# Layers 2 and 3's constants moved from VectorE to GpSimd and ScalarE, and two units' layer-1 attention split by batch, in a four-layer graph kernel

## The chip, the core and the metric

One core of one Trainium2 chip. The metric is the device time of one execution in microseconds. In the profile PE is TensorE's matmuls, PEld its weight loads, DVE is VectorE, ACT ScalarE, POOL GpSimd and SP the sync engine, which here only issues DMAs. L12 is line 12 of the kernel before.

## What is computed

`x` is (64, 256, 128) in float32: 64 batches of 256 nodes with 128 features. `adj` is one symmetric 256x256 matrix of zeros and ones. Four layers follow, each `x = layernorm(x + layer(x))`, all in float32.

```python
# layer 0
h = x @ others_weight;  e = leaky_relu(u1[idx1] + u2[idx2], 0.1)   # u1 = h@a1, u2 = h@a2
out = softmax(where(adj > 0, e, -9e15), axis=1) @ h + x @ self_weight
# layer 1
h = x @ W;  e = leaky_relu(h@a_src + (h@a_dst).T, 0.2)
out = elu(softmax(where(adj + I == 0, -1e9, e)) @ h)
# layer 2: five gated steps; in_matrix = out_matrix = adj
m = adj @ h;  av = concat(m, m);  u3 = h @ u3_w.T + u3_b
z = sigmoid(av @ w3_w.T + w3_b + u3);  r = sigmoid(av @ w4_w.T + w4_b + u3)
hv = tanh(av @ w5_w.T + w5_b + (r*h) @ u5_w.T + u5_b);  h = (1-z)*h + z*hv
# layer 3: y = sum of adj^k x, k = 0..3, twice (adj0 = adj1 = adj), each with its own weight
```

## The kernel before

The batches are taken in 32 units of two (`UB = 2`). A unit's working tile is 128 partitions by 512 values. Ten units are in flight at once, each in a lane with its own SBUF tiles; eight PSUM banks of 128x512 are shared.

No engine's order of work is written by hand. Every instruction is handed to a planner with `add(engine, ns, function, reads, writes)`, where `ns` is a guess of its duration. `Plan.run` plays the engines forward in time on these guesses: when an engine comes free it takes, of the instructions whose inputs are there by the plan, the one with the smallest key. The key (`first`, L996) is the unit's number times 43 us plus the instruction's due time within the unit; due times are the guessed durations and latencies along the unit, stretched by `PACE` (3.1; 1.56 in layer 2). Constants have a rank instead: 0, `R2 = 1` or `R3 = 1.5` times 43 us. The order that comes out is fixed in the program; on the chip each engine goes through its own list in order and waits where an input is late.

Constants (L338 to L498) are made by the same queues while the first units begin: `adjT` (transposed adjacency), `neg0` and `mask1` for the softmaxes; then, of rank R2, the gate weights `gs` (three sums and a difference, L438 and L441) which TensorE transposes into `gT` (L442), the biases `bias2` (L446, L448), the adjacency in another node order `adj_p` (L452), and `fast_blocks` (L461), which makes from `adjTp` and from `adjT` eight 128x128 blocks each, four of them copied (L469) and four of them sums and differences (L471, L474, L475). `left_fast` (L798) multiplies with these blocks, seven products in place of eight. Of rank R3 are layer 3's weights `w3` (L484, L486).

Layer 0 (L620): `x` must lie features by nodes. For units below `XDIRECT = 8` it is loaded as it stands and turned by four TensorE transposes and a ScalarE copy (`feature_major`, L520); later units are loaded by four DMAs in a pattern that one VectorE transpose (L625) turns. A row of attention terms must reach all partitions: for units below `DIRECT_ROWS = 3`, `on_all` (L557) does that with four TensorE transposes into PSUM, later units write a row to DRAM and read it back to all partitions; the same choice decides how the term `d` is made (four one-column products at L663, or two DMAs at L654). Then come masked scores (L669 to L677), their maxima (L679, and `s` at L682), Exp with row sums (L687), the scaling of `h` (L696 for units 0 to 3) and the products L709 and L714, then a layernorm: statistics on VectorE (L577), a power on GpSimd (L582), the scaling (L603 to L613).

Layer 1 (L727): four Prelus on ScalarE (L733, one for each batch and half of the nodes), one Exp over both batches (L736), one multiply with `mask1` over both (L737), the products L744 into one bank, one ScalarE copy (L747), the products L757, reciprocals and scaling (L761 to L768), elu (L774 to L786), layernorm. After unit 0's last scaling, six dummy products (`warm`) are planned at the lowest rank.

Layer 2 (L846) has TensorE's largest share: five products of 512 columns in each of its steps (L868), and `left_fast` (L811) or the plain product (L794). Layer 3 (L948) has L969 and L976.

The helper `small` (L510) sends some short instructions of units from `TIGHT = 4` up to GpSimd, those named in `SMALL`, with a planned 220 ns, and the others to VectorE.

Of the kernel before, what the change touches and what calls it, by code (L numbers as in the profile page):

```python
# [9 lines left out]
AF = mybir.ActivationFunctionType  # L10
# [3 lines left out]
P = 128  # L14
# [7 lines left out]
FAST = (1, 2, 3, 4, 5)  # L22
NORM = (0, 1, 2, 3)
SCALES = True
SMALL = ("ve", "cu", "d", "s", "elu", "shift")
TIGHT = 4
FIRST_FAR = {0: 2, 1: 2}
LAST_FAR = {0: 1}
PERIOD = 43e3
TAIL = 0.3  # L30
LATE = 6
PACE = 3.1
PACE_GATED = 1.56
HOLD = 80
DIRECT_ROWS = 3
XDIRECT = 8
START = 35e3
R2 = 1
R3 = 1.5
# [158 lines left out]
def kernel(  # L198
# [28 lines left out]
    nc = tc.nc  # L227
# [207 lines left out]

    gs = [cell(f"gs{k}", [D, D]) for k in range(3)]
    for k in range(3):
        add(DVE, 250, lambda k=k: nc.vector.tensor_add(gs[k].ap, gates[k].ap[:, 0, :], gates[k].ap[:, 1, :]),  # L438
            (gates[k],), (gs[k],))

    add(DVE, 250, lambda: nc.vector.tensor_sub(gs[0].ap, gs[0].ap, gs[1].ap), (gs[0], gs[1]), (gs[0],))  # L441
# [6 lines left out]
    add(DVE, 150, lambda: nc.vector.tensor_scalar_mul(bias2.ap[:, 0:2], bias2.ap[:, 0:2], 0.5), (bias2,), (bias2,))  # L448
# [12 lines left out]
    def fast_blocks(name, mat):  # L461


        f = cell(name, [P, 2 * NC, N])

        def block(k):
            return f.ap.rearrange("p k (c n) -> p (k c) n", c=NC)[:, k]

        add(DVE, 420, lambda: nc.vector.tensor_copy(f.ap[:, 0:NC], mat.ap), (mat,), (f,))  # L469
        for out, (i, op, j) in {4: (1, ALU.subtract, 0), 6: (3, ALU.add, 1), 5: (6, ALU.subtract, 0)}.items():  # L470
            add(DVE, 250, lambda out=out, i=i, op=op, j=j: nc.vector.tensor_tensor(block(out), block(i), block(j), op=op),  # L471
                (f,), (f,))

        add(DVE, 250, lambda: nc.vector.tensor_scalar_mul(block(5), block(5), -1.0), (f,), (f,))  # L474
        add(DVE, 250, lambda: nc.vector.tensor_add(block(7), block(5), block(2)), (f,), (f,))  # L475
        return f

    adjTf = fast_blocks("adjTf", adjTp)
# [2 lines left out]

    plan.rank = R3
    w3 = cell("w3", [D, 2, 2, D])
    add(DVE, 250, lambda: nc.vector.tensor_add(w3.ap[:, 0, 0, :], wk.ap[:, :, 0], ident.ap), (wk, ident), (w3,))  # L484
# [85 lines left out]
    def layernorm(u, L, pairs, swap=False, centred=False, last=False):  # L570
# [14 lines left out]
        if by_act and not centred:  # L585
            mean = st.ap.rearrange("p k (j s) -> p k j s", j=2)[:, :, :, 1]
            if "shift" in SMALL:
                add(POOL, 220, lambda: nc.gpsimd.tensor_scalar_mul(
                    nm.ap.rearrange("p (k j) -> p k j", k=2), mean, -1.0), (st,), (nm,))
                add(POOL, 220, lambda: nc.gpsimd.tensor_mul(ve.ap, nm.ap, rstd.ap), (nm, rstd), (ve,))  # L590
# [136 lines left out]
    def layer1(u, L):  # L727
        H = D + 1
        esd, e, p = L["esd"], L["e"], L["p"]
        es, ev = on_all(u, L["m"], L["row"], esd, lambda: esd.ap[:, 0])  # L730
        for g in range(G):
            b = g // NC
            add(ACT, 600, lambda g=g, b=b: nc.scalar.activation(  # L733
                e.ap[:, g, :].rearrange("p (c n) -> p c n", c=NC), ev()[:, b], AF.Prelu, bias=esd.ap[:, 1, g : g + 1], alpha=0.2), (es, esd), (e,), group=es)
        ef, pf = e.ap.rearrange("p g n -> p (g n)"), p.ap.rearrange("p g n -> p (g n)")
        add(ACT, 950, lambda: nc.scalar.activation(ef, ef, AF.Exp), (e,), (e,))  # L736
        add(DVE, 1150, lambda: nc.vector.tensor_mul(  # L737
            p.ap.rearrange("p (b c) n -> p b (c n)", b=UB), e.ap.rearrange("p (b c) n -> p b (c n)", b=UB),
            mask1.ap.rearrange("p (o c) n -> p o (c n)", o=1).to_broadcast([P, UB, NC * N])), (e, mask1), (p,))

        ps_x, px = bank(), L["xT0"]
        for b in range(UB):
            for jc in range(NC):
                add(PE, mm_ns(N), lambda b=b, jc=jc: nc.tensor.matmul(  # L744
                    ps_x.ap[:, b * N : (b + 1) * N], X[u].ap[:, b, jc, :], p.ap[:, b * NC + jc, :],
                    start=(b == 0 and jc == 0), stop=(jc == NC - 1), skip_group_check=True), (X[u], p), (ps_x,))
        add(ACT, 500, lambda: nc.scalar.copy(px.ap, ps_x.ap), (ps_x,), (px,))  # L747
        rs, hp, hn, th = L["rs"], L["ht"], L["m"], L["th"]
        ex, parts = L["ex"], object()
        for b in range(UB):  # L750
            ps_o = bank()

            def ov(ps_o=ps_o):
                return ps_o.ap[:, 0 : NC * H].rearrange("p (c k) -> p c k", c=NC)

            for ic in range(NC):
                add(PE, mm_ns(H), lambda b=b, ic=ic, ov=ov: nc.tensor.matmul(  # L757
                    ov()[:, ic, :], bn(px.ap)[:, b, ic * P : (ic + 1) * P], wx1.ap,
                    start=(ic == 0), stop=True, skip_group_check=True), (px, wx1), (ps_o,))
            r = rs.ap[:, b * NC : (b + 1) * NC].rearrange("p (c o) -> p c o", o=1)  # L760
            add(DVE, 120, lambda r=r, ov=ov: nc.vector.reciprocal(r, ov()[:, :, D : D + 1]), (ps_o,), (rs,), group=parts)  # L761
            for c in range(NC if SCALES and u >= TIGHT else 0):
                add(ACT, 290, lambda b=b, c=c, ov=ov: nc.scalar.activation(
                    gd(hp.ap)[:, b * NC + c, :], ov()[:, c, 0:D], AF.Copy, scale=rs.ap[:, b * NC + c : b * NC + c + 1]),
                    (ps_o, rs), (hp,), group=parts)
            if not SCALES or u < TIGHT:
                add(DVE, 350, lambda b=b, r=r, ov=ov: nc.vector.tensor_mul(
                    gd(hp.ap)[:, b * NC : (b + 1) * NC, :], ov()[:, :, 0:D], r.to_broadcast([P, NC, D])), (ps_o, rs), (hp,), group=parts)  # L768
# [267 lines left out]
```

## Time and profile before

| | us |
|---|---|
| median of 7 runs | 1400.63 |
| lowest and highest | 1399.58, 1401.84 |
| the profiled execution's own time | 1400.57 |
| its span in the profile | 1398.8 |
| TensorE busy in the span | 1385.7 |
| VectorE busy | 1206.2 |
| ScalarE busy | 932.7 |
| GpSimd busy | 281.7 |

The span runs from the first instruction to the last of the profiled execution. The granted TensorE clock was 0.999 of full speed. The DMA queues moved 147.05 MB. A row of the groups by line reads: line, engine, operation, tiles written and read, shapes, count, busy us, mean ns, and the idle time of that engine just before these instructions with what ended most of it. "x8" of a float32 matmul is four matmuls, since each is recorded twice, while a transpose is recorded once.

### The profile page before, as it was taken

What the parts mean: (1) busy time and instruction counts of PE and PEld (TensorE: products, weight loads), DVE (VectorE), ACT (ScalarE), POOL (GpSimd) and SP (SyncE); (2) the same over time, 40 slices, a digit from 0 to 9 for tenths busy, and PEclk for the clock granted to TensorE, in tenths of its full rate; (3) what the DMA queues carried; (4) which work ended last, traced back from release to release, by engine and by line L of the source; (5) the groups of instructions that cost most, each with busy time, mean ns of one, the idle gap of its engine ahead of it and who ended that gap; (6) DMA issues with size and microseconds to landing.
All of it is one profiled execution on the core that took longest, in us unless ns stands there. A gap on an engine that the chain in (4) does not pass through costs nothing.

```text
span 1398.8 us, 21934 instructions
## 1 busy us (share of the span) xinstructions
PE 1385.7 (99%) x6529; PEld 962.5 (69%) x6529; DVE 1206.2 (86%) x2849; ACT 932.7 (67%) x2147; POOL 281.7 (20%) x526
## 2 busy tenths in 40 slices
PE   8999999999999999999999999999999999999998
PEld 8767676767666666676766676776666666666776
DVE  7978898989989989889889898899789888899853
ACT  5897756465675767766676678788765546565543
POOL 0312011112212212221221221133112011112212
PEclk9999999999999999999999999999999999999999
DMA  4214455445545544555445645545454443455512
GB/s 118 64 38 101 98 113 126 93 103 121 123 100 119 117 106 103 125 110 117 111 102 115 128 99 124 112 106 126 94 121 115 101 107 85 108 119 120 116 45 53
DMA packets 533254, 147.05 MB, mean 105 GB/s; under 512 B 460688, under 2 KB 498320, under 8 KB 533136
## 3 DMA queue, kind: packets, MB, share of 16 engines
q1 hardware_dynamic: 532336, 145.13, 46.3%
q8 instruction: 52, 0.85, 0.3%
q14 instruction: 66, 0.54, 0.1%
q10 hardware_dynamic: 800, 0.52, 0.1%
HBM read 81.10 MB, written 64.46 MB: 104 GB/s over the span
## 4 chain that ended last, share of the span: by engine, by line
PE 96%; DVE 2%; ACT 1%; issue 0%; POOL 0%; ACTq 0%; POOLq 0%; DVEq 0%
PE ps L868 48%; PE ps L811 17%; PE ps L969 8%; PE ps L794 5%; PE ps L744 4%; PE ps L714 4%; PE ps L976 4%; PE ps L757 2%; PE ps L709 2%; PE ps L638 2%; ACT p L687 0%; PE ps L345 0%; DVE e L669 0%; PE ps L523 0%; PE ps L933 0%
## 5 line engine op out<-in xcount | busy, mean ns | idle before, releaser
L868 PE MATMUL ps<-m,gT 128*128 128x512 f32 x960 | 462.6, 592 | 0.0
L868 PEld LDWEIGHTS ps<-m,gT 128*128 128x128 f32 x960 | 171.9, 190 | 127.0 <-issue 104.9
L887 ACT ACTIVATE e<-ps,bias 128x512 f32<-128x512 f32 x160 | 110.6, 691 | 122.3 <-PE ps L868 122.0
L879 ACT ACTIVATE e<-ps,bias 128x512 f32<-128x512 f32 x160 | 110.2, 689 | 104.2 <-PE ps L868 102.6
L582 POOL TENSOR_TENSOR rstd<-ve,nhalf 128x4 f32<-128x4 f32 x128 | 144.9, 1133 | 94.0 <-DVE ve L579 91.3
L868 PE MATMUL ps<-e,u5T 128*128 128x512 f32 x320 | 162.9, 592 | 0.0
L811 PEld LDWEIGHTS ps<-adjTf,ht 128*128 128x128 f32 x726 | 115.8, 191 | 65.6 <-issue 55.0
L579 POOL TENSOR_SCALAR ve<-st 128x4 f32<-128x4 f32 x112 | 36.2, 323 | 589.1 <-DVE st L577 543.4
L811 PE MATMUL ps<-adjTf,e 128*128 128x128 f32 x968 | 138.4, 275 | 0.0
L896 ACT ACTIVATE p<-ps,bias 128x512 f32<-128x512 f32 x160 | 110.0, 689 | 42.5 <-PE ps L868 39.3
L811 PEld LDWEIGHTS ps<-adjTf,e 128*128 128x128 f32 x968 | 125.4, 192 | 13.6 <-issue 11.6
L811 PE MATMUL ps<-adjTf,ht 128*128 128x128 f32 x726 | 122.4, 274 | 0.0
L898 DVE SCALAR_TENSOR_TENSOR p<-e,p 128x512 f32<-128x512 f32 x160 | 109.3, 684 | 14.2 <-ACT p L896 13.7
L868 PEld LDWEIGHTS ps<-e,u5T 128*128 128x128 f32 x320 | 59.6, 190 | 65.8 <-issue 52.1
L868 PE MATMUL ps<-xT,gT 128*128 128x512 f32 x192 | 97.4, 593 | 0.0
L838 DVE TENSOR_TENSOR m<-ps,e 128x256 f32<-128x256 f32 x152 | 63.4, 417 | 39.1 <-PE ps L811 36.2
L733 ACT ACTIVATE e<-m,esd 128x256 f32<-128x256 f32 x116 | 83.4, 766 | 0.7 <-DMA m<-row 0.7
L823 ACT COPY e<-ps 128x128 f32<-128x128 f32 x152 | 39.9, 266 | 55.1 <-PE ps L811 50.7
L536 DVE STREAM_TRANSPOSE p<-x 128x512 f32<-128x512 f32 x61 | 67.5, 1106 | 7.5 <-ACT x L603 7.0
L577 DVE BATCH_NORM_STATS2 st<-ps 128x6 f32<-128x256 f32 x128 | 51.9, 423 | 25.1 <-PE ps L976 15.0
L841 DVE TENSOR_TENSOR m<-ps,m 128x256 f32<-128x256 f32 x152 | 63.1, 417 | 11.0 <-PE ps L811 9.3
L714 PEld LDWEIGHTS ps<-ht,p 128*128 128x128 f32 x512 | 64.7, 190 | 11.4 <-issue 10.8
(189 smaller groups left out, 2904.1 us busy)
## 6 DMA issues: line engine op xcount, KB each, us to landing
hb<-p SPq DMA_DIRECT2D x182, 256.0 KB, 2.3
ht<-hb SPq DMA_DIRECT2D x484, 64.0 KB, 2.5
xT<-hb SPq DMA_DIRECT2D x244, 64.0 KB, 2.6
m<-row SPq DMA_DIRECT2D x58, 256.0 KB, 3.8
hb<-p SPq DMA_DIRECT2D x124, 64.0 KB, 1.8
ht<-hb SPq DMA_DIRECT2D x31, 256.0 KB, 3.1
out_dram<-x SPq DMA_DIRECT2D x29, 256.0 KB, 2.4
m<-in_x_dram SPq DMA_DIRECT2D x96, 64.0 KB, 2.3
```

The costliest lines, as they stand in the source:

```text
L536: add(DVE, 1050, lambda: nc.vector.transpose(v.ap.rearrange("p (a g i) -> p g a i", g=G, i=BL), X[u].ap.rearrange("p b c (j a) -> p (b c) ...
L582: add(POOL, 1050, lambda: nc.gpsimd.tensor_tensor(rstd.ap, ve.ap, nhalf.ap, op=ALU.pow), (ve, nhalf), (rstd,))
L714: add(PE, mm_ns(D + 2), lambda b=b, ic=ic, kc=kc, yv=yv: nc.tensor.matmul(yv()[:, ic, :], p.ap[:, b * NC + kc, ic * P : (ic + 1) * P], h.a ...
L733: add(ACT, 600, lambda g=g, b=b: nc.scalar.activation(e.ap[:, g, :].rearrange("p (c n) -> p c n", c=NC), ev()[:, b], AF.Prelu, bias=esd.ap ...
L794: add(PE, mm_ns(N), lambda b=b, mc=mc: nc.tensor.matmul(ps.ap[:, b * N : (b + 1) * N], lhs(b, mc), mat.ap[:, mc, :], start=(mc == 0), stop ...
L811: add(PE, mm_ns(P) + 4, lambda: nc.tensor.matmul(ps.ap[:, at * P : (at + 1) * P], lhs(), mat.ap[:, k, c * P : (c + 1) * P], start=True, st ...
L868: add(PE, mm_ns(T), lambda: nc.tensor.matmul(ps.ap, w(), rhs.ap, start=start, stop=stop, skip_group_check=True), (c, rhs), (ps,), after)
L879: add(ACT, 600, lambda ps_g=ps_g, up=up: nc.scalar.activation(r.ap, ps_g.ap, AF.Tanh, bias=bias2.ap[:, 1:2], scale=0.5 / up), (ps_g, bias2 ...
L887: add(ACT, 600, lambda ps_g=ps_g, up=up: nc.scalar.activation(z.ap, ps_g.ap, AF.Tanh, bias=bias2.ap[:, 0:1], scale=0.5 / up), (ps_g, bias2 ...
L896: add(ACT, 600, lambda ps_v=ps_v, up=up: nc.scalar.activation(v.ap, ps_v.ap, AF.Tanh, bias=bias2.ap[:, 2:3], scale=1 / up), (ps_v, bias2), ...
L898: add(DVE, 600, lambda: nc.vector.scalar_tensor_tensor(v.ap, z.ap, 1.0, v.ap, op0=ALU.add, op1=ALU.mult), (v, z), (v,))
L969: add(PE, mm_ns(N), lambda k=k, src=src, c=c, b=b: nc.tensor.matmul(view(c)[:, :, b, :], bn(src.ap)[:, b, c * P : (c + 1) * P], w3.ap[:, k ...
```

## The change

Four parts, and the planner's numbers with them.

1. The 22 instructions that make `gs`, `bias2`, the summed blocks of `fast_blocks` and `w3` are on GpSimd instead of VectorE; the three copies (`adj_p`, and the first half of each `fast_blocks`) are on ScalarE.
2. In layer 1, units 0 and 1 (`HALVES = 2`) go batch by batch: Prelus, Exp, mask, products, copy for batch 0, then for batch 1, each batch with a PSUM bank of its own. Other units do as before.
3. `s` (L682) is no longer in `SMALL`, so it is on VectorE for all units. `DIRECT_ROWS` is 4 instead of 3 and `XDIRECT` 9 instead of 8: unit 3 gets its rows and `d` by TensorE, unit 8 its `x` by TensorE.
4. `PACE` is 2.8 instead of 3.1, and the planned costs of short GpSimd instructions rise from 220 to 250, 280 or 300 ns.

```diff
-SMALL = ("ve", "cu", "d", "s", "elu", "shift")
+SMALL = ("ve", "cu", "d", "elu", "shift")
+HALVES = 2
-PACE = 3.1
+PACE = 2.8
-DIRECT_ROWS = 3
-XDIRECT = 8
+DIRECT_ROWS = 4
+XDIRECT = 9
...
-        add(DVE, 250, lambda k=k: nc.vector.tensor_add(gs[k].ap, gates[k].ap[:, 0, :], gates[k].ap[:, 1, :]),
+        add(POOL, 480, lambda k=k: nc.gpsimd.tensor_add(gs[k].ap, gates[k].ap[:, 0, :], gates[k].ap[:, 1, :]),
...
-        add(DVE, 150, lambda k=k, j=j: nc.vector.tensor_add(
+        add(POOL, 270, lambda k=k, j=j: nc.gpsimd.tensor_add(
...
-    add(DVE, 600, lambda: nc.vector.tensor_copy(
+    add(ACT, 600, lambda: nc.scalar.copy(
         adj_p.ap, adj_t.ap.rearrange("p i (m q j) -> p (i m) j q", m=NC, j=BL)), (adj_t,), (adj_p,))
...
-        add(DVE, 420, lambda: nc.vector.tensor_copy(f.ap[:, 0:NC], mat.ap), (mat,), (f,))
+        add(ACT, 500, lambda: nc.scalar.copy(f.ap[:, 0:NC], mat.ap), (mat,), (f,))
...
-            add(DVE, 250, lambda out=out, i=i, op=op, j=j: nc.vector.tensor_tensor(block(out), block(i), block(j), op=op),
+            add(POOL, 480, lambda out=out, i=i, op=op, j=j: nc.gpsimd.tensor_tensor(block(out), block(i), block(j), op=op),
...
-        add(DVE, 350, lambda k=k: nc.vector.tensor_add(
+        add(POOL, 480, lambda k=k: nc.gpsimd.tensor_add(
             w3.ap[:, k % 2, k // 2, :], wk.ap[:, :, k], wk.ap[:, :, k + 3]), (wk,), (w3,))
...
-        add(POOL if pool else DVE, 220 if pool else ns, lambda: op(nc.gpsimd if pool else nc.vector), reads, writes, **more)
+        add(POOL if pool else DVE, 300 if pool else ns, lambda: op(nc.gpsimd if pool else nc.vector), reads, writes, **more)
...
+        for bs in [[b] for b in range(UB)] if u < HALVES else [list(range(UB))]:
+            n = len(bs)
+            ec, pc = (e, p) if n == UB else ((L["r"], L["v"]), (L["z"], L["xT1"]))[bs[0]]
...
+            add(ACT, 115 + 418 * n, lambda at=at: nc.scalar.activation(e.ap[:, at], e.ap[:, at], AF.Exp), (ec,), (ec,))
+            add(DVE, 50 + 550 * n, lambda at=at, n=n: nc.vector.tensor_mul(
...
+            ps_x = bank()
...
+            add(ACT, 80 + 210 * n, lambda bs=bs, n=n, ps_x=ps_x: nc.scalar.copy(
+                px.ap[:, bs[0] * N : bs[0] * N + n * N], ps_x.ap[:, 0 : n * N]), (ps_x,), (px,), group=copies)
```

The same moves are made for the lines that are left out (the difference `gs`, the scaling of `bias2`, the negation and the last sum of `fast_blocks`, the first block of `w3`). Within a batch of layer 1 the products and the scaling are the lines of before.

More of the change, by code (lines that the diff above doesn't have):

```diff
@@ L437 @@
     for k in range(3):
-        add(DVE, 250, lambda k=k: nc.vector.tensor_add(gs[k].ap, gates[k].ap[:, 0, :], gates[k].ap[:, 1, :]),
+        add(POOL, 480, lambda k=k: nc.gpsimd.tensor_add(gs[k].ap, gates[k].ap[:, 0, :], gates[k].ap[:, 1, :]),
             (gates[k],), (gs[k],))
-    add(DVE, 250, lambda: nc.vector.tensor_sub(gs[0].ap, gs[0].ap, gs[1].ap), (gs[0], gs[1]), (gs[0],))
+    add(POOL, 480, lambda: nc.gpsimd.tensor_sub(gs[0].ap, gs[0].ap, gs[1].ap), (gs[0], gs[1]), (gs[0],))
     gT = transposed("gT", [(gs[0], gs[0].ap), (gs[1], gs[1].ap), (gs[2], gs[2].ap), (u3, u3.ap)])
@@ L445 @@
     for k, j in enumerate((3, 3, 4)):
-        add(DVE, 150, lambda k=k, j=j: nc.vector.tensor_add(
+        add(POOL, 270, lambda k=k, j=j: nc.gpsimd.tensor_add(
             bias2.ap[:, k : k + 1], biases.ap[:, k : k + 1], biases.ap[:, j : j + 1]), (biases,), (bias2,))
-    add(DVE, 150, lambda: nc.vector.tensor_scalar_mul(bias2.ap[:, 0:2], bias2.ap[:, 0:2], 0.5), (bias2,), (bias2,))
+    add(POOL, 300, lambda: nc.gpsimd.tensor_scalar_mul(bias2.ap[:, 0:2], bias2.ap[:, 0:2], 0.5), (bias2,), (bias2,))
     adjTp, adj_p = cell("adjTp", [P, NC, N]), cell("adj_p", [P, NC * NC, BL, P // BL])
-    add(DVE, 600, lambda: nc.vector.tensor_copy(
+    add(ACT, 600, lambda: nc.scalar.copy(
         adj_p.ap, adj_t.ap.rearrange("p i (m q j) -> p (i m) j q", m=NC, j=BL)), (adj_t,), (adj_p,))
@@ L467, in block @@
             return f.ap.rearrange("p k (c n) -> p (k c) n", c=NC)[:, k]
-        add(DVE, 420, lambda: nc.vector.tensor_copy(f.ap[:, 0:NC], mat.ap), (mat,), (f,))
+        add(ACT, 500, lambda: nc.scalar.copy(f.ap[:, 0:NC], mat.ap), (mat,), (f,))
         for out, (i, op, j) in {4: (1, ALU.subtract, 0), 6: (3, ALU.add, 1), 5: (6, ALU.subtract, 0)}.items():
-            add(DVE, 250, lambda out=out, i=i, op=op, j=j: nc.vector.tensor_tensor(block(out), block(i), block(j), op=op),
+            add(POOL, 480, lambda out=out, i=i, op=op, j=j: nc.gpsimd.tensor_tensor(block(out), block(i), block(j), op=op),
                 (f,), (f,))
-        add(DVE, 250, lambda: nc.vector.tensor_scalar_mul(block(5), block(5), -1.0), (f,), (f,))
-        add(DVE, 250, lambda: nc.vector.tensor_add(block(7), block(5), block(2)), (f,), (f,))
+        add(POOL, 350, lambda: nc.gpsimd.tensor_scalar_mul(block(5), block(5), -1.0), (f,), (f,))
+        add(POOL, 480, lambda: nc.gpsimd.tensor_add(block(7), block(5), block(2)), (f,), (f,))
         return f
@@ L483 @@
     w3 = cell("w3", [D, 2, 2, D])
-    add(DVE, 250, lambda: nc.vector.tensor_add(w3.ap[:, 0, 0, :], wk.ap[:, :, 0], ident.ap), (wk, ident), (w3,))
+    add(POOL, 480, lambda: nc.gpsimd.tensor_add(w3.ap[:, 0, 0, :], wk.ap[:, :, 0], ident.ap), (wk, ident), (w3,))
     for k in range(1, 4):
-        add(DVE, 350, lambda k=k: nc.vector.tensor_add(
+        add(POOL, 480, lambda k=k: nc.gpsimd.tensor_add(
             w3.ap[:, k % 2, k // 2, :], wk.ap[:, :, k], wk.ap[:, :, k + 3]), (wk,), (w3,))
@@ L587, in layernorm @@
             if "shift" in SMALL:
-                add(POOL, 220, lambda: nc.gpsimd.tensor_scalar_mul(
+                add(POOL, 280, lambda: nc.gpsimd.tensor_scalar_mul(
                     nm.ap.rearrange("p (k j) -> p k j", k=2), mean, -1.0), (st,), (nm,))
-                add(POOL, 220, lambda: nc.gpsimd.tensor_mul(ve.ap, nm.ap, rstd.ap), (nm, rstd), (ve,))
+                add(POOL, 250, lambda: nc.gpsimd.tensor_mul(ve.ap, nm.ap, rstd.ap), (nm, rstd), (ve,))
             else:
@@ L730, in layer1 @@
         es, ev = on_all(u, L["m"], L["row"], esd, lambda: esd.ap[:, 0])
[L731 to L768, printed above, removed]
@@ new lines, in layer1, with ov @@
+        px, rs, hp, hn, th, ex = (L[name] for name in ("xT0", "rs", "ht", "m", "th", "ex"))
+        parts, copies = object(), object()
+        for bs in [[b] for b in range(UB)] if u < HALVES else [list(range(UB))]:
+            n = len(bs)
+            ec, pc = (e, p) if n == UB else ((L["r"], L["v"]), (L["z"], L["xT1"]))[bs[0]]
+            at = slice(bs[0] * NC, (bs[-1] + 1) * NC)
+            for b in bs:
+                for g in range(b * NC, (b + 1) * NC):
+                    add(ACT, 600, lambda g=g, b=b: nc.scalar.activation(
+                        e.ap[:, g, :].rearrange("p (c n) -> p c n", c=NC), ev()[:, b], AF.Prelu,
+                        bias=esd.ap[:, 1, g : g + 1], alpha=0.2), (es, esd), (ec,), group=es)
+            add(ACT, 115 + 418 * n, lambda at=at: nc.scalar.activation(e.ap[:, at], e.ap[:, at], AF.Exp), (ec,), (ec,))
+            add(DVE, 50 + 550 * n, lambda at=at, n=n: nc.vector.tensor_mul(
+                p.ap[:, at].rearrange("p (b c) n -> p b (c n)", b=n), e.ap[:, at].rearrange("p (b c) n -> p b (c n)", b=n),
+                mask1.ap.rearrange("p (o c) n -> p o (c n)", o=1).to_broadcast([P, n, NC * N])), (ec, mask1), (pc,))
+            ps_x = bank()
+            for k, b in enumerate(bs):
+                for jc in range(NC):
+                    add(PE, mm_ns(N), lambda b=b, jc=jc, k=k, ps_x=ps_x: nc.tensor.matmul(
+                        ps_x.ap[:, k * N : (k + 1) * N], X[u].ap[:, b, jc, :], p.ap[:, b * NC + jc, :],
+                        start=(k == 0 and jc == 0), stop=(jc == NC - 1), skip_group_check=True), (X[u], pc), (ps_x,))
+            add(ACT, 80 + 210 * n, lambda bs=bs, n=n, ps_x=ps_x: nc.scalar.copy(
+                px.ap[:, bs[0] * N : bs[0] * N + n * N], ps_x.ap[:, 0 : n * N]), (ps_x,), (px,), group=copies)
+            for b in bs:
+                ps_o = bank()
+                def ov(ps_o=ps_o):
+                    return ps_o.ap[:, 0 : NC * H].rearrange("p (c k) -> p c k", c=NC)
+                for ic in range(NC):
+                    add(PE, mm_ns(H), lambda b=b, ic=ic, ov=ov: nc.tensor.matmul(
+                        ov()[:, ic, :], bn(px.ap)[:, b, ic * P : (ic + 1) * P], wx1.ap,
+                        start=(ic == 0), stop=True, skip_group_check=True), (px, wx1), (ps_o,))
+                r = rs.ap[:, b * NC : (b + 1) * NC].rearrange("p (c o) -> p c o", o=1)
+                add(DVE, 120, lambda r=r, ov=ov: nc.vector.reciprocal(r, ov()[:, :, D : D + 1]), (ps_o,), (rs,), group=parts)
+                for c in range(NC if SCALES and u >= TIGHT else 0):
+                    add(ACT, 290, lambda b=b, c=c, ov=ov: nc.scalar.activation(
+                        gd(hp.ap)[:, b * NC + c, :], ov()[:, c, 0:D], AF.Copy, scale=rs.ap[:, b * NC + c : b * NC + c + 1]),
+                        (ps_o, rs), (hp,), group=parts)
+                if not SCALES or u < TIGHT:
+                    add(DVE, 350, lambda b=b, r=r, ov=ov: nc.vector.tensor_mul(
+                        gd(hp.ap)[:, b * NC : (b + 1) * NC, :], ov()[:, :, 0:D], r.to_broadcast([P, NC, D])),
+                        (ps_o, rs), (hp,), group=parts)
```

## The prediction

> **What bounds the kernel.** I read the page's engine shares first, then the chain that ended last, then the busy table by stretches of the start, then TensorE's waits, and last the timeline around the longest of those waits.
>
> ```profile
> PE 1385.7 (99%) x6529; PEld 962.5 (69%) x6529; DVE 1206.2 (86%) x2849; ACT 932.7 (67%) x2147; POOL 281.7 (20%) x526
> PE 96%; DVE 2%; ACT 1%; issue 0%; POOL 0%; ACTq 0%; POOLq 0%; DVEq 0%
> 10.00:20.00 10.00, 9.28 (x79) 8.64 (x79) 8.05 (x36) 6.17 (x20) 0.00 (x0) 1.00 0.80 193
> 20.00:30.00 10.00, 8.28 (x72) 7.85 (x71) 9.11 (x32) 6.59 (x20) 1.24 (x2) 1.00 0.10 17
> 30.00:40.00 10.00, 10.00 (x80) 9.71 (x79) 9.54 (x30) 7.28 (x24) 3.73 (x7) 1.00 0.21 28
> 40.00:50.00 10.00, 8.89 (x48) 6.95 (x48) 9.09 (x31) 7.29 (x21) 4.29 (x7) 1.00 0.31 85
> ```
>
> The columns of the stretches are PE, PEld, DVE, ACT and POOL busy us, granted clock, DMA share, GB/s. TensorE is busy 99% and carries 96% of the last chain; VectorE's 86% is no bound of the whole. Only in the first 60 us does TensorE have gaps, and there VectorE is at 8 to 9.5 of 10 us while POOL does almost nothing.
>
> A busy TensorE could still run slowly, so I looked at the distance between the starts of consecutive matmuls: 112 ns for 128 columns, 216 for 256, 429 for 512, everywhere (in the timeline, eight L709 matmuls take 0.89 us and eight L969 ones 1.73). Those distances, summed over all 6529 matmuls, are about 1381 us. So the span is work 1381, plus about 3 us before the first DMA lands (four dummy products run there anyway), some stalls, and about 6.8 us from the last matmul (1392.0) to the end (1398.8). The stalls, from the same starts, are 5.6 us between 4.4 and 60 us and 3.3 us in all that follows (the largest 1.36 us at 338.6). No engine speedup can win more than these 8.9 us unless it takes TensorE work away.
>
> ```profile
> PE ps L744 <- DVE p L737: 2.8, 2, 1.7
> PE ps L345 <- POOL ident masks.py:199: 1.3, 1, 1.3
> PE ps L757 <- ACT xT L747: 1.2, 1, 1.2
> PE ps L523 <- DVE adjf L471: 0.4, 1, 0.4
> PE ps L523 <- DMA m<-in_x_dram: 0.3, 1, 0.3
> ```
>
> The waits name the line (total us, times, longest). The largest is L744, layer 1's first product, behind the mask multiply L737: once for unit 0 and once for unit 1. Its run-up in the timeline, unit 0:
>
> ```profile
> 25.54 1.57 ACT L733 ACTIVATE e<-ps,esd 128x256 f32<-128x256 f32 x4 [0.28 <-ACT ht L641]
> 27.14 1.06 ACT L736 ACTIVATE e<-e 128x1024 f32<-128x1024 f32 x1
> 28.40 1.22 DVE L737 TENSOR_TENSOR p<-e,mask 128x1024 f32<-128x1024 f32 x1
> 29.67 1.99 PE L744 MATMUL ps<-p,x 128*128 128x256 f32 x8 [1.72 <-DVE p L737]
> ```
>
> Four Prelus, one Exp over both batches, one multiply over both, and only then may TensorE start: 4.1 us in series.
>
> **The change, part by part.**
>
> *Halves, units 0 and 1.* One batch needs two Prelus (0.79), an Exp of 512 (0.62, row L780), a multiply of 512 (two-input row L786: 0.69): from 25.54 the first product could start near 27.75 instead of 29.67. TensorE came free at 27.8, so that stall of 1.98 us (with its 0.1 us of refill) goes, and what is late next is the second batch: ScalarE is through its Exp near 28.4, VectorE near 29.1, while the first batch's four matmuls end near 28.6. I leave 0.45 us of stall: saved 1.5. At 46.15, unit 1, the stall was 1.37; by the same arithmetic I leave 0.3: saved 1.1. The price is a shorter second instruction of each kind: two Exps for one, 2 x 0.62 - 1.06 = 0.18 us per unit; two multiplies, 2 x 0.69 - 1.22 = 0.16; two PSUM copies, 2 x 0.38 (row L641, 266 columns) - 0.58 = 0.18. All of it lies within the shorter series above. TensorE's matmuls stay the same.
>
> *Constants.* 25 VectorE instructions leave: by the busy column L438 0.8, L441 0.3, L446 and L448 0.6, L452 0.6, L469 0.8, L471 1.8, L474 0.4, L475 0.6, L484 and L486 1.4, together 7.3 us, all between 5.5 and 26.9 us. ScalarE takes three 512-wide copies, about 0.6 each (row L378): 1.8 us, in stretches where it is 3.5 to 6.2 of 10 us busy; without that cover they would cost at most 1.8 on the way to the first layer. POOL takes 22. The trace has no 128x128 two-input POOL instruction: the nearest row below is the one-input select of the identity at 0.29 us, the longest POOL row of any kind is 2.71 (L582). I take 0.5 for each of 18 wide ones, near the lower row because beside no other work POOL's rows lie at their minima, and 0.2 for the four bias ones: 10 us, between 8 and about 25 us, where POOL was busy 1.2 us. First uses: gT at 45.7, adjTf at 99.6, adjf at 162, w3 at 175.6, so 20 us of cover at least, except that gs is transposed on TensorE at 15.2, in order. Behind these on POOL stands rstd L582 of unit 0 at 21.8; at most one 0.5 us instruction stands before it.
> What does 7.3 us less on VectorE bring? Not 7.3. Between 10 and 20 us the first unit's series is latency: VectorE is 8 of 10 us busy and the instructions that stand in its way there are a 0.4 copy at 11.4, gT at 15.9, a bias and a block at 17.4. TensorE's stalls at 16.1 and 17.0 (0.48 and 0.56) and the small ones (about 1.3 with that near 58) are what can be won; I take 0.7 and 0.4 of them. Bounds: nothing, and 2.3.
>
> *Unit 3's rows by TensorE.* Added: four transposes for layer 0 and four for layer 1, 8 x 0.112 = 0.9 us, and four one-column products (eight records; 24 records took 2.3 us) 0.8. Removed: seven SP DMAs with their two round trips (L550, L554, L654), 1.2 us of ScalarE (L733 from PSUM 474 ns against 762 from SBUF, four times), 0.4 of VectorE (L669 417 against 608, twice). *Unit 8's x by TensorE:* four transposes 0.45 us and a 0.59 ScalarE copy, against a 0.69 VectorE transpose and four SP issues that become one. TensorE's total grows by 2.1 us, and since it is the bound, this is paid in full unless it fills a stall that would have stayed; VectorE and SP gain where they are not the limit.
>
> *s back on VectorE for units 4 up.* 56 POOL instructions of a median 556 ns go, 56 of 227 ns come to VectorE, 12.7 us over the run, of which 2.7 for units 4 to 9 before 90 us.
>
> ```profile
> L682 POOL TENSOR_SCALAR s<-top,d x56: 259/556/1815, 45.7 to 1229.3; 128x2 f32<-128x2 f32 x56
> L682 DVE TENSOR_SCALAR s<-top,d x8: 223/226/234, 12.2 to 44.7; 128x2 f32<-128x2 f32 x8
> ```
>
> Minimum, median and longest: POOL's instruction stretches beside VectorE, VectorE's does not. Cost nothing: TensorE has no stall between 59 and 250 us. Without that cover it would be up to 2.7.
>
> *The planner's numbers* (PACE 2.8, POOL costs 250 to 300). They reorder every queue. The 3.3 us of later stalls are places where the written order and the real times differ; I keep 3.3, between nothing and twice that. The end of 6.8 us is a fixed series of statistics, power, scaling and store.
>
> **Sum.** The profiled execution took 1400.57, its span 1398.8, so 1.8 lies around it; the median is 1400.63. 1400.6 - 1.5 - 1.1 - 0.7 - 0.4 + 2.1 = 1399.0.
>
> **The rivals.**
> *More is won.* All 5.6 us at the start go and a third of the later 3.3: 1400.6 - 5.6 - 1.1 + 2.1 = 1396.0. For it: every stall at the start stands behind VectorE, ScalarE or a late load, all relieved. Against: each unit 2 up still has the unsplit series (stall of 0.35 at 57.5).
> *GpSimd is late, slower.* TensorE takes its instructions in order, and the transposes of gs (L364) are written in near 15 us. If the six or so POOL instructions up to gs take 1.8 us each (the longest L682) instead of 0.5, TensorE stands 6 x 1.3 = 8 us: 1399.0 + 8 = 1407. It ends slower than before by 0.2% once they take over about 1.25 us each. Against: the long POOL rows lie beside dense two-input VectorE work such as L737 and L898, of which little is left before 15 us.
> *VectorE is held by GpSimd.* Beside POOL work VectorE's rows keep their length (L898 684 ns with, 685 without), but POOL's were tiny there. If all 18 wide ones held VectorE for their 0.5, it would lose 9 and win 7.3: the stalls stay and the series grows by 1.7: 1400.6 + 2.1 + 1.7 = 1404.4; it turns from gain to loss where 7.3 us are lost. The Trainium skill, SBUF — State Buffer, "Who interferes with whom", says that a VectorE instruction with two SBUF inputs or in a two-port mode and a GpSimd one that reads SBUF exclude each other for the whole instruction, whichever starts first; the stretched POOL rows agree with one half of that, and no row here shows the other half.
> *The new order is worse.* Later stalls double: 1399.0 + 3.3 = 1402.3; triple: 1405.6. Against: the POOL costs in the plan come nearer to the rows (220 before, median 556).
>
> **Chances.** Forecast 0.52, more won 0.31, GpSimd late 0.04, VectorE held 0.04, worse order 0.09. A measurement of this kernel can tell about 0.2%, 2.8 us: faster is under 1397.8, slower over 1403.4. Faster: 0.31 and 0.03 of the forecast's lower edge, 0.34; slower: 0.08 and half of the worse order, 0.12; same 0.54. The range, 1395.3 to 1402.6, takes in the bounds of the start (all of it gone, none of the rest) and the worse order once; it leaves out the two GpSimd cases and its tripling.
>
> **What would show it.** Halves right: L744's wait behind the multiply under 1 us for units 0 and 1 and its first start near 27. Constants right: POOL about 10 us busy before 30 us, VectorE's share there lower, rows near 0.5. TensorE's extra work: 20 more matmul records. The stalls to 60 us near 2 us. It would be wrong if the gs transposes had a wait on POOL, or if L757 or L868 in later stretches had waits that sum to more than 5 us.

## The result, and the profile after

The changed kernel takes 1396.54 us in the median (1395.85 to 1398.13, 14 runs), the kernel before 1400.55 (34 runs): ratio 0.9973, 95% interval 0.9966 to 0.998. That is 4.0 us faster where 1.6 was forecast; 1399.0 was predicted in a range of 1395.3 to 1402.6. The profiled execution's span fell from 1398.8 to 1394.9.

From here on, views of the changed kernel and of those made from it have the lines of that kernel: a line up to layer 1 (L727) stands one further down (L687 is L688), layer 1's L733, L736, L737, L744, L747 and L757 are L741, L744, L745, L752, L755 and L764, and what follows in layers 2 and 3 is eight further down (L868 is L876). Kernels made from the kernel before keep its lines, except before_halves_only, which has those of the changed kernel.

The page of the changed kernel, its engines and its last chain:

```profile
PE 1386.4 (99%) x6549; PEld 965.7 (69%) x6549; DVE 1208.4 (87%) x2880; ACT 937.0 (67%) x2155; POOL 257.3 (18%) x492
PE 99%; ACT 0%; POOL 0%; DVE 0%; issue 0%; ACTq 0%; POOLq 0%; DVEq 0%
```

The 20 added matmul records are there, and VectorE's 2% of the last chain is gone (the share of the span that each engine has in the chain of work that ended last). The stretches of its start (PE, PEld, DVE, ACT, POOL busy us, clock, DMA share, GB/s):

```profile
10.00:20.00 10.00, 9.87 (x87) 9.54 (x87) 8.73 (x27) 6.07 (x19) 8.15 (x20) 1.00 0.84 213
20.00:30.00 10.00, 9.70 (x85) 9.41 (x84) 7.59 (x28) 6.50 (x21) 1.03 (x1) 1.00 0.00 1
30.00:40.00 10.00, 10.00 (x74) 9.56 (x73) 9.42 (x32) 7.99 (x22) 3.37 (x5) 1.00 0.01 2
40.00:50.00 10.00, 10.00 (x46) 7.04 (x46) 5.47 (x18) 7.93 (x25) 0.39 (x2) 1.00 0.16 36
```

TensorE is nearly full from 10 us on and POOL has taken the constants. VectorE is less busy than before from 20 to 30 us (7.59 instead of 9.11) but not from 10 to 20 (8.73 instead of 8.05). All waits of TensorE that its table names, in the whole run:

```profile
PE ps L346 <- POOL ident masks.py:199: 1.3, 1, 1.3
PE ps L664 <- ACT ht L642: 0.3, 1, 0.3
```

The first is the start, before any work. Every other wait of the kernel before is gone, those late in the run too (L757 behind L747). Busy time in long stretches shows the same: TensorE fills all 1320 us, where before it had 239.90, 298.71, 400.00 and 379.74.

```profile
60.00:300.00 240.00, 240.00 (x1112) 164.44 (x1111) 218.66 (x528) 165.01 (x372) 31.45 (x49) 1.00 0.42 94
300.00:600.00 300.00, 300.00 (x1400) 205.78 (x1399) 266.75 (x630) 208.99 (x487) 60.40 (x107) 1.00 0.52 113
600.00:1000.00 400.00, 400.00 (x1909) 280.15 (x1908) 355.56 (x831) 303.46 (x706) 81.87 (x163) 1.00 0.53 114
1000.00:1380.00 380.00, 380.00 (x1703) 256.53 (x1702) 319.20 (x735) 214.86 (x475) 61.18 (x122) 1.00 0.44 100
```

**One account for all kernels.** I take from each trace the distance between the starts of consecutive matmuls and subtract the usual one of its form (111.5 ns for 128 columns, 112 for 129 and 130, 113.5 for 133, 216 for 256, 429.3 for 512, and 118 for up to two columns). What is left is stall; it is summed from 7.3 us, where the clock is full in every profile, and the sum is split at 62 us. The usual distances alone are TensorE's work, and the tail runs from the last matmul to the end. Before: work 1381.0, stalls 5.3 to 62 us and 2.8 later, tail 6.5. After: 1383.3, 0.7, 0 (-0.1), 6.9. (The prediction's 5.6 and 3.3 counted only the gaps over 60 ns of the same list.) The change in span is therefore +2.3 - 4.6 - 2.9 + 0.4, and +0.9 in the first 7.3 us, where the granted clock of this one execution was half until 6.8 us and that of the kernel before until 4.4 (see the end): -3.9. Without these first microseconds the account would give -4.8; the medians differ by 4.0.

### The profile page after: what moved, and what is told of

The parts are those of the page before. It is cut to its first block, busy times and chain, and to the rows that moved or that the text cites. A ratio compares the mean times of both kernels' runs of the same rounds, so it can differ in the third digit from the quotient of the medians.

```text
span 1394.9 us, 21958 instructions
## 1 busy us (share of the span) xinstructions
PE 1386.4 (99%) x6549; PEld 965.7 (69%) x6549; DVE 1208.4 (87%) x2880; ACT 937.0 (67%) x2155; POOL 257.3 (18%) x492
## 4 chain that ended last, share of the span: by engine, by line
PE 99%; ACT 0%; POOL 0%; DVE 0%; issue 0%; ACTq 0%; POOLq 0%; DVEq 0%
PE ps L876 49%; PE ps L819 17%; PE ps L977 8%; PE ps L802 5%; PE ps L715 4%; PE ps L752 4%; PE ps L984 4%; PE ps L764 2%; PE ps L710 2%; PE ps L639 2%; PE ps L346 0%; PE ps L524 0%; PE ps L567 0%; PE ps L941 0%; PE ps L664 0%; ACT p L688 0%
## 5 line engine op out<-in xcount | busy, mean ns | idle before, releaser
L876 PE MATMUL ps<-m,gT 128*128 128x512 f32 x960 | 464.3, 592 | 0.0
L876 PEld LDWEIGHTS ps<-m,gT 128*128 128x128 f32 x960 | 171.5, 190 | 119.9 <-issue 97.5
L876 PE MATMUL ps<-e,u5T 128*128 128x512 f32 x320 | 163.1, 592 | 0.0
L906 DVE SCALAR_TENSOR_TENSOR p<-e,p 128x512 f32<-128x512 f32 x160 | 109.5, 685 | 11.0 <-ACT p L904 10.1
L876 PEld LDWEIGHTS ps<-e,u5T 128*128 128x128 f32 x320 | 59.9, 190 | 61.0 <-issue 47.1
L876 PE MATMUL ps<-xT,gT 128*128 128x512 f32 x192 | 96.7, 593 | 0.0
L741 ACT ACTIVATE e<-m,esd 128x256 f32<-128x256 f32 x112 | 80.7, 766 | 0.0
L890 DVE SCALAR_TENSOR_TENSOR e<-e,xT 128x512 f32<-128x512 f32 x96 | 65.4, 682 | 13.6 <-ACT e L887 12.2
L715 PEld LDWEIGHTS ps<-ht,p 128*128 128x128 f32 x512 | 66.0, 190 | 9.1 <-issue 7.7
```

Source lines behind the costliest of these rows:

```text
L715: add(PE, mm_ns(D + 2), lambda b=b, ic=ic, kc=kc, yv=yv: nc.tensor.matmul(yv()[:, ic, :], p.ap[:, b * NC + kc, ic * P : (ic + 1) * P], h.a ...
L741: add(ACT, 600, lambda g=g, b=b: nc.scalar.activation(e.ap[:, g, :].rearrange("p (c n) -> p c n", c=NC), ev()[:, b], AF.Prelu, bias=esd.ap ...
L876: add(PE, mm_ns(T), lambda: nc.tensor.matmul(ps.ap, w(), rhs.ap, start=start, stop=stop, skip_group_check=True), (c, rhs), (ps,), after)
L906: add(DVE, 600, lambda: nc.vector.scalar_tensor_tensor(v.ap, z.ap, 1.0, v.ap, op0=ALU.add, op1=ALU.mult), (v, z), (v,))
```

## The experiments

All twelve together; ratios to the kernel before, with 95% intervals. "Late" is after 62 us.

| kernel | work | stalls to 62 | late stalls | tail | median | ratio |
|---|---|---|---|---|---|---|
| before | 1381.0 | 5.3 | 2.8 | 6.5 | 1400.55 | |
| after | 1383.3 | 0.7 | -0.1 | 6.9 | 1396.54 | 0.9973 (0.9966 to 0.998) |
| pace_back | 1383.3 | 0.8 | 6.5 | 6.3 | 1402.8 | 1.0017 (1.0008 to 1.0025) |
| pace_279 | 1383.3 | 0.8 | 2.2 | 6.9 | 1399.01 | 0.9989 (0.998 to 0.9998) |
| no_halves | 1383.3 | 1.1 | 9.1 | 6.9 | 1406.23 | 1.0044 (1.0032 to 1.0057) |
| rows_by_dma | 1381.0 | 2.4 | 3.8 | 7.0 | 1400.14 | 1.0001 (0.9992 to 1.001) |
| const_on_vector_same_order | 1383.3 | 2.3 | 0.4 | 6.9 | 1399.07 | 0.9989 (0.998 to 0.9998) |
| const_on_vector_replanned | 1383.3 | 3.6 | 3.7 | 6.9 | 1402.8 | 1.0017 (1.0008 to 1.0025) |
| dummies_left_out | 1380.7 | 3.3 | 0.2 | 6.9 | 1397.49 | 0.9978 (0.9969 to 0.9987) |
| s_on_gpsimd_same_order | 1383.3 | 0.7 | 0.8 | 6.9 | 1396.88 | 0.9975 (0.9965 to 0.9984) |
| before_pace_309 | 1381.0 | 5.2 | 7.2 | 6.4 | 1404.79 | 1.0029 (1.0018 to 1.004) |
| before_const_moved_same_order | 1381.0 | 3.8 | 2.8 | 6.6 | 1400.12 | 0.9995 (0.9986 to 1.0004) |
| before_const_moved_replanned | 1381.0 | 2.8 | 4.7 | 6.5 | 1400.29 | 0.9997 (0.9988 to 1.0006) |
| before_halves_only | 1381.0 | 4.3 | 1.1 | 6.5 | 1398.68 | 0.9987 (0.9979 to 0.9996) |

In every row the median is the sum of work, stalls and tail plus 4.9 to 6.4 us, which is the start, the halved clock and what lies around the span. So the account, from one profile of each kernel, carries the medians, which lie 10 us apart, to within 0.8 us either way.

### Is a late stall a matter of what runs where, or of the order?

```diff
-PACE = 2.8
+PACE = 3.1
```

> The changed kernel with PACE 3.1 again; everything else as changed. Theory A (the late stalls went because GpSimd lost s and the plan's costs fit the chip better): the pace does not matter, stalls after 62 us stay under 0.7 us, time 1396.5 within 0.7. Theory B (the late stalls are a matter of where each newly planned order happens to misjudge): a new order brings a new number, 1 to 4 us of late stalls, time 1397.5 to 1400. The start is the same by both: stalls between 7 and 62 us under 1.5.

Measured: the start as after (0.8), late stalls 6.5, 1402.8 us, slower than before, and beyond theory B's bounds (4 us, 1400) too. TensorE's waits and its long stretches in this kernel:

```profile
PE ps L876 <- DVE m L852: 1.3, 2, 0.9
PE ps L977 <- ACT e L895: 1.2, 1, 1.2
PE ps L819 <- ACT e L831: 0.6, 1, 0.6
```

```profile
60.00:300.00 240.00, 237.48 (x1087) 162.08 (x1086) 215.85 (x523) 167.48 (x378) 33.94 (x50) 1.00 0.43 94
300.00:600.00 300.00, 299.45 (x1404) 205.35 (x1403) 266.39 (x628) 203.09 (x475) 57.52 (x106) 1.00 0.51 112
```

No engine has more to do than after; TensorE waits in places where it did not. Theory A falls. B, with wider bounds, is what two changes without meaning of their own then tested:

```diff
-PACE = 2.8
+PACE = 2.79
```

> The changed kernel with PACE 2.79 in place of 2.8, a change that means nothing by itself but gives another order. Theory A (the change as such ended the late stalls): late stalls under 1 us, time 1396 to 1397.5. Theory B (each order is a draw): late stalls anywhere from 0.5 to 9 us, as in the four orders so far (before 2.8, pace back 6.5, no halves 9.1, rows by DMA 3.8), time 1397 to 1405; the start under 1.5 us of stalls by both.

Measured: late stalls 2.2, 1399.01. The kernel before with the like change:

```diff
-PACE = 3.1
+PACE = 3.09
```

> The kernel before with PACE 3.09 in place of 3.1. Theory A (the late stalls of before are a property of its s on GpSimd and its plan costs): late stalls 2 to 4 us as before, time 1400 to 1401.5. Theory B (each order is a draw): late stalls anywhere from 0.5 to 9, time 1398 to 1407. The stalls before 62 us stay at 5 or so by both, since the first units' order hardly depends on the pace.

Measured: late stalls 7.2 where before had 2.8, 1404.79. The first units keep their stalls (5.2). A third of a per cent in a planning constant moves the time by 2.5 us on one kernel and 4.2 on the other; the whole change moved it by 4.0.

The other way round, with the order kept and the engine changed:

```diff
-        small(u, "s", 130, lambda eng, b=b: eng.tensor_scalar(
+        add(DVE, 130, lambda b=b: (nc.gpsimd if u >= TIGHT else nc.vector).tensor_scalar(
```

> The changed kernel in its own order, with s run on GpSimd for units 4 up (still planned on VectorE). Theory A (s on GpSimd is what made late stalls): late stalls of 1 us or more come back, time 1397.5 or above. Theory B (a given order keeps its late stalls, whatever runs s): late stalls under 0.6, time 1396.0 to 1397.3.

Measured: late stalls 0.8, between the two bounds, and 1396.88, inside B's range and no different from after within the intervals. `s` did run on GpSimd, and one of its 56 took 1308 ns:

```profile
L683 POOL TENSOR_SCALAR s<-top,d x56: 261/268/1308, 59.0 to 1222.5; 128x2 f32<-128x2 f32 x56
```

So which engine runs `s` is worth 0.9 us of late stalls in these two profiles and 0.3 us between the medians. Over the ten orders that I ran, late stalls were -0.1, 1.1, 2.2, 2.8, 3.7, 3.8, 4.7, 6.5, 7.2 and 9.1; over the kernels that kept an order they stayed near that order's (-0.1, 0.2, 0.4 and 0.8 for after's, 2.8 and 2.8 for before's). Late stalls belong to the order. Nor does the change seem to bring better ones: the six orders made from the changed kernel have 4.2 us in the mean, the four made from the kernel before 4.0. That the changed kernel itself got the lowest of the ten is luck, as far as these runs tell.

### The split by batch

```diff
-HALVES = 2
+HALVES = 0
```

> The changed kernel with HALVES 0: units 0 and 1 have one Exp and one multiply over both batches again. Theory A (the prediction's sum): the two stalls of L744 come back, about 2.6 us, time 1399. Theory B (the first start of that product was only 0.18 us earlier after the change, and TensorE had other products in between): the split is worth under 1 us, time 1396.5 to 1397.5, with stalls before 62 us under 1.7.

Measured: stalls to 62 us only 1.1, so 0.4 more than after: theory B for the start. The time, 1406.23, is beyond both theories: this is a new order too, with late stalls of 9.1, one of them 4.6 long, within which the clock was halved (the loss by that is in the 9.1). The largest wait, and the stretches around it (PE busy us, granted clock, DMA share, GB/s):

```profile
PE ps L819 <- DVE e L814: 4.4, 1, 4.4
```

```profile
295.00:300.00 5.00, 1.28 (x6) 0.88 0.52 109
300.00:305.00 5.00, 4.32 (x13) 0.50 0.68 179
```

In the timeline VectorE had work without a break from 296.1 to 300.5 (transposes, gates of other units), and the L814 for which TensorE stood came last in that list.

The split alone, in the kernel before:

```diff
+HALVES = 2
...
+        for bs in [[b] for b in range(UB)] if u < HALVES else [list(range(UB))]:
```

> The kernel before with the split by batch for units 0 and 1 alone, newly planned. Theory A (the prediction's sum): L744's stalls at 27.7 and 46.2 shrink by 2.6 us in all, stalls before 62 us 2.7. Theory B (the split matters little, what filled these stalls is other work of TensorE): stalls before 62 us 4 or more. The late stalls are a draw by the runs so far (0 to 9), so the time, 1396 to 1405, tells less than the stalls.

Measured: stalls to 62 us 4.3, so 1.0 saved and not 2.6; theory B (in a new order again: a split kernel has more instructions, so it can't keep the old one). The time 1398.68 has 1.7 less of late stalls in it. The timeline of unit 0 in this kernel:

```profile
25.94 1.57 ACT L741 ACTIVATE e<-ps,esd 128x256 f32<-128x256 f32 x4 [0.28 <-ACT ht L642]
27.38 1.16 ACT L744 ACTIVATE e<-e 128x512 f32<-128x512 f32 x2
28.38 1.28 DVE L745 TENSOR_TENSOR p<-e,mask 128x512 f32<-128x512 f32 x2
29.11 1.56 PE L752 MATMUL ps<-p,x 128*128 128x256 f32 x6 [0.76 <-DVE p L745]
```

All four Prelus run first, then both Exps, then both multiplies: the planner did not put batch 0 ahead of batch 1. From the first Prelu to the first product it is 3.2 us instead of 4.1. The stall at 28 shrank from 1.98 to 1.02, the one at 46 went, and 2.5 us of others came between 51 and 56.

### The constants

VectorE with the constants again, in after's order:

```diff
-        add(POOL, 480, lambda k=k: nc.gpsimd.tensor_add(gs[k].ap, gates[k].ap[:, 0, :], gates[k].ap[:, 1, :]),
+        add(POOL, 480, lambda k=k: nc.vector.tensor_add(gs[k].ap, gates[k].ap[:, 0, :], gates[k].ap[:, 1, :]),
...
```

> The changed kernel in its own planned order, but the 22 GpSimd constants and the three ScalarE copies run on VectorE (they are still planned as GpSimd's and ScalarE's, so all other instructions keep their order). VectorE has 7.3 us more before 27 us. Theory A (VectorE's load sets the start): 2 to 4 us of stalls come back before 62 us, time 1398.5 to 1400.5. Theory B (the start is latency and order, VectorE's load is covered): under 1 us, time 1396.5 to 1397.5.

Measured: 2.3 us of stalls to 62 us, 1.6 more than after, between the two theories (2 to 4, under 1) and nearer to A's; 1399.07, inside A's range. And the constants moved in before's order:

```diff
-        add(DVE, 250, lambda k=k: nc.vector.tensor_add(gs[k].ap, gates[k].ap[:, 0, :], gates[k].ap[:, 1, :]),
+        add(DVE, 250, lambda k=k: nc.gpsimd.tensor_add(gs[k].ap, gates[k].ap[:, 0, :], gates[k].ap[:, 1, :]),
...
```

> The kernel before in its own order, with the 25 constants run on GpSimd and ScalarE (still planned as VectorE's, so the rest keeps its order). Theory A (VectorE's load at the start is worth what putting it back cost after the change, 1.6 us of stalls before 62 us): stalls before 62 us 3.3 to 4.3 instead of 5.3, time 1398.5 to 1399.7. Theory B (VectorE is held by GpSimd's wide instructions and gets little): stalls 5 or more, time 1400 to 1401.

Measured: stalls 3.8, 1.5 less, as A said; the time, 1400.12, is not: it lies in B's range, 0.4 under before, and its interval includes no change. The two swaps agree on the stalls, to 0.1 us: the load alone is worth 1.5 us of them. In time the one showed 2.5 us and the other 0.4. The rest of the stalls went with a new plan:

```diff
-    add(DVE, 600, lambda: nc.vector.tensor_copy(
+    add(ACT, 600, lambda: nc.scalar.copy(
...
-        add(DVE, 250, lambda k=k: nc.vector.tensor_add(gs[k].ap, gates[k].ap[:, 0, :], gates[k].ap[:, 1, :]),
+        add(POOL, 480, lambda k=k: nc.gpsimd.tensor_add(gs[k].ap, gates[k].ap[:, 0, :], gates[k].ap[:, 1, :]),
...
```

> The kernel before with the constants on GpSimd and ScalarE and planned there, nothing else changed. Moving them within the old order took 1.5 us off the stalls before 62 us. Theory A (the move pays mainly because the planner then writes unit 1's layer 0 earlier in all queues): the stalls before 62 us fall to 1 to 2.5, and unit 1's first Exp L687 starts near 22 instead of 28.1. Theory B (only VectorE's time counts): 3.5 to 4, as within the old order. Late stalls a draw, time 1396 to 1404.

Measured: stalls 2.8, so 2.5 saved, a little above A's band; unit 1's first Exp L687 starts at 21.04, as A said. Its late stalls, 4.7, give the gain back: 1400.29. And the whole change but this part:

```diff
-    add(ACT, 600, lambda: nc.scalar.copy(
+    add(DVE, 600, lambda: nc.vector.tensor_copy(
...
-        add(POOL, 480, lambda k=k: nc.gpsimd.tensor_add(gs[k].ap, gates[k].ap[:, 0, :], gates[k].ap[:, 1, :]),
+        add(DVE, 250, lambda k=k: nc.vector.tensor_add(gs[k].ap, gates[k].ap[:, 0, :], gates[k].ap[:, 1, :]),
...
```

> The changed kernel with its constants on VectorE as before and planned there. Theory A (the earlier order for unit 1 comes with the constants' move): stalls before 62 us 3 to 4.5, more than the 2.3 in the unchanged order, and unit 1's first Exp is late, 25 or after. Theory B (the order comes from something else): 2.3 or less. Late stalls a draw, time 1397 to 1405.

Measured: stalls 3.6, unit 1's first Exp at 28.8, a stall before unit 0's L752 as long as the old one (1.87 at 29.2) although that kernel has the split; 1402.8 with late stalls of 3.7. Theory A. But the engine that TensorE waits for is now ScalarE:

```profile
PE ps L752 <- ACT ht L642: 1.7, 1, 1.7
```

```profile
28.71 1.28 DVE L745 TENSOR_TENSOR p<-e,mask 128x512 f32<-128x512 f32 x2
30.77 1.50 ACT L642 COPY ht<-ps 128x266 f32<-128x266 f32 x5
```

Both multiplies are over at 29.99, and L752 starts at 31.20. The copy L642 stands on ScalarE behind unit 1's four late Exps (28.80 to 30.77). L752 doesn't read `ht`, so what it waits for is presumably the PSUM bank that this copy reads; that is not shown. The first Exp of unit 1, first the row of before, then that of after:

```profile
28.11 0.49 ACT L687 ACTIVATE p<-e,nm 128x256 f32<-128x256 f32 x1
```

```profile
21.70 0.51 ACT L688 ACTIVATE p<-e,nm 128x256 f32<-128x256 f32 x1 [2.56 <-DVE nm L686]
```

The four orders with the old place for the constants have it at 28.1 to 28.8 (before, pace 3.09, halves only, constants back and replanned), the six planned with the new place at 21.0 to 21.9. With unit 1's scores done 6.4 us earlier, TensorE has its products to do while unit 0's mask is multiplied. After, around unit 0's first product:

```profile
25.54 1.57 ACT L741 ACTIVATE e<-ps,esd 128x256 f32<-128x256 f32 x4
26.19 1.95 PE L715 MATMUL ps<-ht,p 128*128 128x130 f32 x16
26.99 1.16 ACT L744 ACTIVATE e<-e 128x512 f32<-128x512 f32 x2
28.63 1.27 DVE L745 TENSOR_TENSOR p<-e,mask 128x512 f32<-128x512 f32 x2
29.04 0.62 PE L639 MATMUL ps<-wx,xT 128*128 128x133 f32 x4
29.49 1.89 PE L752 MATMUL ps<-p,x 128*128 128x256 f32 x8
```

L752 starts 0.18 us earlier than L744 did before, hardly a change. But L715 of unit 1 stands at 26.2, before L752, where TensorE used to wait.

### TensorE's added and idle work

```diff
-DIRECT_ROWS = 4
-XDIRECT = 9
+DIRECT_ROWS = 3
+XDIRECT = 8
```

> The changed kernel with DIRECT_ROWS 3 and XDIRECT 8: 20 matmul records, 2.1 us of TensorE, go. Theory A (TensorE's added work is paid in full): time 1394.4 if no stall comes back, 1395.5 with a stall of 1 us for unit 3's rows by DMA. Theory B (that work filled stalls that would have stayed): the stalls before 62 us grow by 2 us or more and the time is 1396.5 or above.

Measured: 2.3 us of work less, 1.7 of start stalls more, late stalls 3.8; 1400.14. Between the theories, nearer to B at the start (1.7, where B said 2 or more): stalls of three quarters of the added work's size come back (the waits are L752 behind the mask, and L941). Both parts of the added work left together and the order is new, so which of the two fills what is not shown. The six dummy products:

```diff
-            warm(6, [plan.tasks[-1]])
+            warm(6, [plan.tasks[-1]], issue=False)
```

This kernel plans them and leaves them out.

> The changed kernel in its own order, with the six dummy products planned but not issued (they compute nothing that is used). Theory A (TensorE is the bound without a gap now, so its work is paid in full): 6 x 0.43 = 2.6 us less, 1394.0, with stalls before 62 us as after, under 1. Theory B (the dummies stand where TensorE would wait anyway): the stalls before 62 us grow by 1.5 or more and the time is 1395.5 to 1396.5.

Measured: 2.6 us of work less, 2.6 of start stalls more, as theory B said; 1397.49, above B's range, but no different from after within the intervals. After, and then without them (whose largest wait is L524 for the layer-1 output of unit 0):

```profile
37.66 2.75 PE L346 MATMUL ps<-ident 128*128 128x256 f32 x12
40.25 0.27 PE L524 MATMUL ps<-ident,x 128*128 128x128 f32 x1
```

```profile
PE ps L524 <- DVE x L612: 1.5, 1, 1.5
```

A TensorE that is full between 30 and 41 us has, after the change, 2.6 us of filling in it: the latency of unit 0's layer 1 still bounds that stretch.

## Why the prediction was right or wrong

The bound was read rightly: only stalls and TensorE's own work move the time, and the account of these carries all fourteen medians. The time lay in the range and moved the way that was forecast, but by 4.0 us and not 1.6: 0.27% (0.20 to 0.34), over the 0.2% from which the prediction counts a kernel as faster, to which it gave 0.34. The time is nearly that of the rival "more is won", 1396.0, and that is luck: the rival took all of the start and a third of the late stalls, and what went was most of the start and all of the late ones. The range's lower edge, 1395.3, doesn't follow from the bounds that it names: with all 5.6 us of the start gone and nothing else the sum is 1400.6 - 5.6 + 2.1 = 1397.1, and 1396.54 lies below that. What carried the time below that is the late stalls, of which the sum had kept all 3.3 us.

- *TensorE's added work*, 2.1 us: measured 2.3.
- *The start*, 3.7 saved: measured 4.6, with the shares wrong, so that the sum is near by errors that offset each other. The halves' 1.5 + 1.1 failed on the step "one batch needs two Prelus, then Exp": all four Prelus run first. The first product starts at 29.49, where the prediction's sign was a start near 27; that its wait is gone is not the split's doing. Alone they save 1.0; taken from the full change, 0.4. The constants' 0.7 (and 0.4) was too small for another reason: I priced VectorE's load, and the load alone is worth 1.5, but moving it also let the planner write unit 1's layer 0 6.4 us earlier (2.5 with the new plan in the kernel before). That removed the very stall that I had given to the halves: it is gone without any split in no_halves and in before_const_moved_replanned. Parts do not add: 2.5 and 1.0 alone, 4.6 together with the rows.
- *Later stalls*, "I keep 3.3": this term failed most; measured 2.8 before by the account used here, and nothing after. It is 2.9 of the 3.9 us in the span. My bounds (nothing to twice, 5.6 by this account) held this case and would not have held pace_back, no_halves or before_pace_309, all of which went beyond. My reason for expecting better orders, costs nearer to the rows, is not borne out: pace_back has the same costs of GpSimd and 6.5.
- *GpSimd's price*, 10 us for 22 instructions: measured 10.1, from 8.8 to 18.2 us. The transposes of `gs` had no wait on POOL in TensorE's table.
- *VectorE held by GpSimd*, a rival at 4%: its mechanism is real, its price small. Six VectorE instructions between 9 and 19 us took together 1.4 us longer than the same forms before. After:

```profile
9.48 0.92 DVE L430 TENSOR_TENSOR mask<-adjT,ident 128x128 f32<-128x128 f32 x2
9.75 1.56 POOL L439 TENSOR_TENSOR gs<-gate 128x128 f32<-128x128 f32 x3
```

```profile
16.45 1.71 POOL L487 TENSOR_TENSOR w<-wk 128x128 f32<-128x128 f32 x3
17.66 1.06 DVE L697 TENSOR_TENSOR ht<-ht,rs 128x520 f32<-128x520 f32 x1
```

The same L697 took 698 ns before (as L696); an L430 took 282 (as L429) and here 456 and 539. The Trainium skill, SBUF — State Buffer, "Who interferes with whom", has both halves of this, and here the trace agrees with both: VectorE waits for a GpSimd instruction in progress (the 456 and 539 above), and GpSimd for VectorE (the third L439, begun during a VectorE instruction, took 634 ns, the other two 498). It cost 1.4 and not 9: only six instructions were held, and each by less than the time of the one GpSimd instruction beside it.
- *s back on VectorE, at nothing*: 56 fewer on POOL, no wait of TensorE on it; the swap within the order moved the median by less than the intervals.

What stays open: why the changed kernel's order has no late stall. It is shown that late stalls go with the order and that orders next to it (PACE 2.79) have 2.2 us; it is not shown that any part of the change makes good orders more likely (4.2 us in the mean with it, 4.0 without), and ten orders are too few to tell. Of the span's 3.9 us, then, 2.3 net are won at the start (4.6 of stalls less 2.3 of work) and 2.9 later, by the order that the change happened to get; the tail (0.4) and the halved clock (0.9) go the other way.

## What to carry to other kernels

Where a planner writes the queues, every edit draws a new order, and the draw (here 0 to 9 us of stalls in 1400) can outweigh the edit: run a change without meaning beside it, and test a part by running it on another engine while it is planned as it was. Price a moved instruction not by its engine's busy time but by what the order lets the bound engine do in the gap. A bound engine that looks full may be full of filling: leave the filling out once and see whether the time moves.

## What the runs showed of the hardware

A 128x128 two-input float32 sum took GpSimd 449 to 452 ns at its shortest (L472; 557 at most) and 590 to 599 for L487, against 285 and 382 on VectorE before. When TensorE stood for 4.6 us (no_halves, 296.1 to 300.7), its granted clock was 0.50 from 298.8 to 305.6, and the distance between its 256-column matmuls there 427 ns instead of 216. No other stall after 10 us, up to 1.9 us, halved the clock. In the 14 profiles the full clock was first granted at 4.4 to 7.3 us, though the first matmul started at 1.35 in all of them. This moves a single profiled span by up to 1.2 us, so it should be taken out before two spans are compared.

The Trainium skill, TensorE: Matmul & The Clock Gate, "Part 1: The HAM clock gate (the "warmup" mystery)", says that the clock falls to half after an idle window of about 3.4 us, that the windows run freely, and that the first full clock varies by 500 ns either way. The trace agrees that the windows run freely: the three stretches between the clock's changes in no_halves, 293.55, 6.83 and 1095.68 us, are 86, 2 and 321 times 3.413 us. It doesn't agree that a whole idle window is needed: the last matmul before the fall started at 296.01, only 2.8 us ahead of it. And the first full clock spreads over 2.9 us, wider than the page gives.
